# Three hand-written instruction orders laid out anew in a conditional residual MLP

## The chip, the cores and the metric

The kernel runs on one core of one Trainium2 chip. The time is that of the device, in microseconds (us), for one execution. Engines are named as the profile names them: PE (matmul), PEld (PE's weight load), DVE (vector), ACT (scalar), POOL (GpSimd) and SP (which issues most of the plain DMAs).

## The reference

For 16 x 512 tokens of width 512 the reference adds to `x` a two-layer MLP with a layer norm. The MLP's input is the concatenation of six modulated copies of the token, 3072 wide:

```python
h = _ln(x, pw_g[pathway_ids], pw_b[pathway_ids])
h = _ln(h, cp_g[compartment_ids], cp_b[compartment_ids])
t = _ln(x, tm_g[time_steps], tm_b[time_steps])
m = x + _mlp_ln(memory_state, ...)[:, None, :]      # one row per sequence; n and r likewise
s = _ln(x, ms_g[scale_type], ms_b[scale_type])
w = jax.nn.softmax(aw)
cat = jnp.concatenate([w[0]*h, w[1]*t, w[2]*m, w[3]*n, w[4]*r, w[5]*s], axis=-1)
return x + _mlp_ln(cat, int_W1, int_b1, int_W2, int_b2, int_g, int_be)   # _mlp_ln: silu(s@W1+b1)@W2+b2, then layer norm
```

`compartment_ids` and `time_steps` are the same array, with values 0 to 4; `scale_type` is an array of 0 and 1; `pathway_ids` runs from 0 to 499.

## The kernel before

**Tiling.** The tokens are sorted into groups by their compartment and scale, and are worked through in 16 groups `w` of 512 tokens, four tiles of 128 each. Layer 1 multiplies three 512-wide inputs of a token: X (the token itself, row sums folded into per-row additions), V (its normalised form, with weights scaled per compartment and scale) and H (the twice normalised form). Each input is transposed by DVE (`turn`, L198) and spread over the partitions by four DMAs of SP (`spread_row`, L206). Layer 2 (Z is its transposed input) runs one group behind layer 1.

**Products.** The V part of a tile is one piece `lV.w.j` (L405, accumulating into a PSUM tile `p`). X and H of two tiles at a time (pair `p`, 0 or 1) go through seven half products `m7.w.p.k` (`half_product`, L453) instead of eight; four sums of their inputs (`u1` to `u4`, `token_sum`, L434 to L440) and four sums of their outputs (`r1`, `r2`, `r3`, `r5`, `half_out`, L462 to L470) belong to them; products 1, 6, 7 and 5 share a PSUM tile `u`. Layer 2 has the same scheme: fourteen sevenths per group, `q7.w.p.k` (`seventh`, L547), which write two PSUM tiles per pair, `pq_0a`, `pq_0b` for p = 0 and `pq_1a`, `pq_1b` for p = 1. Products 1, 6 and 2 go to the a tile, 5, 3, 7 and 4 to the b tile. Between them the partial results are taken out:

```python
def sum_first(st, i):                                   # piece sf.w.i, L564 (even i) and L566 (odd i)
    y, ab, ed = y_halves(st, i // 2)
    if i % 2 == 0:
        nc.vector.tensor_add(y[:, 0], y[:, 0], ab[:, 1])
    else:
        nc.vector.tensor_add(y[:, 3], y[:, 3], ed[:, 1])
```

`kf` (`keep_first`, ACT, L557 and L559) and `ku` (`keep_last`, ACT, L570) copy a half out, `sl` (`sum_last`, DVE, L575 and L577) makes the last sums, `kb` (ACT, L521) puts the bias into a PSUM tile ahead of the first product, `zs` (`z_sums`, POOL, L533 to L539) makes the sums of the products' inputs. In the last group layer 2 runs as plain products, `l2` (L488).

**Other pieces that the text names.** On POOL the gathers of rows by index (L172): `gx` the tokens, `gh` and `gc` two tables, `ga` the additions to layer 1's result; `sh` (L392); `xp` and `fp` powers; `po` (L639) the scatter of the result. On DVE `f1` (L347, L348), `f2` (L384), `th`, `tx`, `tv`, `tz` the transposes of H, X, V and Z (L198), `ha` the addition to layer 1's result (L473), `wz` the half sums of layer 1's weights (L420 to L423), `wq` those of layer 2's (L495 to L498), `bd.w.j` the build of a V block (L266), which runs only where a tile begins a new sort group and is a skipped branch elsewhere (L249), and the last steps `yg` (L585), `la` (L608), `ft` (L604).

**Order.** Nothing schedules the work but three lists of piece names: `ORDER` (the head: preparation, the three small MLPs of the conditions, group 0's layer 1 and the start of group 1), `WINDOW` (the steady group) and `LAST` (the last group). `run` calls the pieces in the list's order, and each engine gets its instructions in that order. `WINDOW` is run 15 times, with c for the current group, p for the one before, n and m for the next two:

```python
for w in range(NW - 1):
    run(WINDOW, w)
run(LAST, NW - 1)
```

Waits between engines are put in by the tiles that a piece reads and writes: an instruction waits for every earlier one, in the list's order, that read or wrote the tile in a way that conflicts. A PSUM tile of 128 x 512 counts as one tile there, also where two instructions touch different halves of it. Where a list names a reader of a tile ahead of the next product into it, the product waits for the reader; where it names it behind, the reader waits for the product.

Of the kernel before, what the change touches and what calls it, by code (L numbers as in the profile page):

```python
# [1549 lines left out]
```

## Time and profile before

| | |
|---|---|
| median of 3 runs | 920.85 us (915.66 to 922.26) |
| span of the profiled execution | 922.1 us, mean granted clock 0.988 |
| PE busy | 886.5 us, 96% |
| DVE busy | 736.2 us, 80% |
| POOL busy | 656.9 us, 71% |
| ACT busy | 524.5 us, 57% |

The span is counted from the first to the last instruction of the profiled execution; all sums below are made against it. A row of a timeline names start, duration, engine, line, operation, what is written and read, and in brackets the idle time of the engine ahead of it and what ended that. A row of the chain names start, duration and the work. Matmul durations reach past the next one's start, since they are pipelined; a matmul's slot is the distance between two starts.

### The profile page before, as it was taken

The page shows a single profiled execution, that of the slowest core. Times are in us where ns is not written, and L with a number is a line of the kernel's source. Part 1 is how long each engine was busy: PE and PEld are TensorE (multiplying, and loading weights), DVE is VectorE, ACT ScalarE, POOL GpSimd, SP SyncE. Part 2 cuts the span into 40 slices and gives each one's busy share as a digit, 9 for nine tenths or more (in the row PEclk, how much of TensorE's full clock was granted, in tenths as well). Part 3 has the DMA queues.
Part 4 walks back from the last instruction along what each step waited for, and adds up shares of the span by engine and source line. Part 5 has one row for each costly group of instructions (what it writes and reads, how often), then busy time and mean ns, then how long its engine had stood idle before and what let it go on. Part 6 is the DMA issues. An engine that isn't in the chain of part 4 may idle for free.

```text
span 922.1 us, 13747 instructions
## 1 busy us (share of the span) xinstructions
PE 886.5 (96%) x3617; PEld 644.0 (70%) x3617; DVE 736.2 (80%) x1360; ACT 524.5 (57%) x1263; POOL 656.9 (71%) x730
## 2 busy tenths in 40 slices
PE   6978998999999999999999999999999999999995
PEld 6634445868777776767687777778686867778682
DVE  8776866878879798978787887969799798979565
ACT  5558735556473738564564647374657566573313
POOL 9867678566867868687777777786768687866352
PEclk9979999999999999999999999999999999999999
DMA  8836687586867767686868676686768696876513
GB/s 273 276 104 204 216 235 215 151 246 169 246 182 215 209 196 223 183 234 190 250 178 244 185 229 200 203 229 194 214 173 246 168 259 174 246 201 181 152 37 111
DMA packets 88558, 185.40 MB, mean 201 GB/s; under 512 B 24324, under 2 KB 24388, under 8 KB 88476
## 3 DMA queue, kind: packets, MB, share of 16 engines
q0 software_dynamic: 31104, 104.88, 39.7%
q1 hardware_dynamic: 56668, 79.53, 29.1%
q8 instruction: 30, 0.49, 0.3%
q14 instruction: 52, 0.43, 0.2%
q10 hardware_dynamic: 704, 0.08, 0.1%
HBM read 100.48 MB, written 19.97 MB: 131 GB/s over the span
## 4 chain that ended last, share of the span: by engine, by line
PE 46%; POOL 4%; issue 3%; DVE 2%; SPq 1%; DMA 1%; POOLq 0%; ACT 0%; DVEq 0%
PE u L453 12%; PE p L405 12%; PE p L453 10%; PE pq_0b L547 4%; PE pq_1b L547 3%; PE pq_0a L547 2%; PE pq_1a L547 2%; POOL out L639 1%; SPq L206 1%; DMA catZ<-rZ 1%; POOL xbs L392 1%; PE p L488 0%; POOL xbs L172 0%; POOL rsh L373 0%; POOL cp L172 0%
## 5 line engine op out<-in xcount | busy, mean ns | idle before, releaser
L405 PE MATMUL p<-vs,catV 128*128 128x512 f32 x512 | 231.9, 596 | 4.3 <-ACT sums L352 3.6
L405 PEld LDWEIGHTS p<-vs,catV 128*128 128x128 f32 x512 | 97.6, 191 | 103.3 <-issue 96.2
L373 POOL TENSOR_TENSOR rsh<-veh,mhalf 128x1 f32<-128x1 f32 x64 | 52.3, 817 | 84.4 <-DVE veh L369 68.8
L453 PE MATMUL p<-wh__81,catH 128*128 128x256 f32 x480 | 110.9, 379 | 0.0
L377 ACT ACTIVATE pw<-pw,rsh 128x512 f32<-128x512 f32 x64 | 46.0, 718 | 104.4 <-DVE pw L384 55.1
L453 PEld LDWEIGHTS p<-wh__81,catH 128*128 128x128 f32 x480 | 91.2, 190 | 12.4
L639 POOL DMA_INDIRECT out<-yb,tok x64 | 67.8, 1059 | 33.5 <-issue 19.4
L172 POOL DMA_INDIRECT pw<-in_pw,i_pw x64 | 63.0, 984 | 34.8 <-DVE veh L369 20.5
L476 ACT ACTIVATE add<-add 128x512 f32<-128x512 f32 x64 | 40.0, 629 | 82.4 <-DVE add L473 55.1
L172 POOL DMA_INDIRECT add<-rows,i_add x64 | 71.6, 1119 | 20.0 <-issue 18.0
L351 ACT ACTIVATE junk<-pw 128x512 bf16<-128x512 f32 x60 | 37.7, 628 | 80.1 <-DVE pw L348 59.3
L392 POOL TENSOR_TENSOR xbs<-xbs,rows 128x512 f32<-128x512 f32 x64 | 82.1, 1285 | 1.2
L172 POOL DMA_INDIRECT xbs<-in_x,tok x64 | 66.8, 1043 | 17.2 <-issue 14.7
L172 POOL DMA_INDIRECT cp<-cp_rows,i_cp x64 | 67.1, 1048 | 16.2 <-issue 13.2
L347 DVE SCALAR_TENSOR_TENSOR pw<-xbs,sums,pw 128x512 f32<-128x512 f32 x60 | 54.1, 902 | 16.8 <-DMA pw<-in_pw,i_pw 14.3
L384 DVE SCALAR_TENSOR_TENSOR pw<-pw,sumsh,cp 128x512 f32<-128x512 f32 x60 | 43.6, 748 | 28.4 <-DMA cp<-cp_rows,i_cp 20.8
L318 ACT ACTIVATE xm<-xbs,nmx,rsx 128x512 f32<-128x512 f32 x64 | 48.8, 807 | 27.0 <-issue 11.0
L453 PEld LDWEIGHTS u<-wx__80,catX 128*128 128x128 f32 x240 | 45.6, 190 | 18.7 <-issue 13.4
L453 PE MATMUL u<-wt,catX 128*128 128x256 f32 x240 | 56.6, 379 | 0.1
L453 PE MATMUL p<-wt,catH 128*128 128x256 f32 x240 | 56.7, 379 | 0.0
L453 PE MATMUL u<-wx__80,catX 128*128 128x256 f32 x240 | 56.7, 379 | 0.0
L453 PE MATMUL u<-wt,ss 128*128 128x256 f32 x240 | 54.4, 379 | 0.0
(439 smaller groups left out, 2098.0 us busy)
## 6 DMA issues: line engine op xcount, KB each, us to landing
catX<-rX SPq DMA_DIRECT2D x240, 64.0 KB
catV<-rV SPq DMA_DIRECT2D x240, 64.0 KB
catZ<-rZ SPq DMA_DIRECT2D x240, 64.0 KB
catH<-rH SPq DMA_DIRECT2D x240, 64.0 KB
rows<-adde SPq DMA_DIRECT2D x8, 256.0 KB
yb<-in_int_W SPq DMA_DIRECT2D x1, 1024.0 KB
catH<-in_int_W SPq DMA_DIRECT2D x1, 1024.0 KB
w1x<-in_int_W SPq DMA_DIRECT2D x1, 1024.0 KB
```

Source lines behind the costliest of these rows:

```text
L172: nc.gpsimd.indirect_dma_start(dst, None, table, bass.IndirectOffsetOnAxis(ap=idx, axis=0), **kw)
L318: nc.scalar.activation(t, st["xb"][:, j, :], AF.Identity, bias=st["nm"][:, j : j + 1], scale=st["rs"][:, j : j + 1])
L347: nc.vector.scalar_tensor_tensor(h, st["xb"][:, j, :], st["sums"][:, 1, j : j + 1], h, ALU.add, ALU.mult)
L373: nc.gpsimd.tensor_tensor(rs, st.pop(("ve", j)), mhalf[:, :1], ALU.pow)
L377: nc.scalar.mul(pw[:, :D], pw[:, :D], st.pop(("rs", j)))
L384: nc.vector.scalar_tensor_tensor(pw[:, :D], pw[:, :D], st["sh", j][:, 1], cp, ALU.add, ALU.mult)
L392: nc.gpsimd.tensor_add(st["xb"][:, j, :], st["xb"][:, j, :], rows[:, 2, :])
L405: nc.tensor.matmul(st["p1", g], st["c" + blk][:, g, c, :], m[:, c, :], start=(blk == first and c == order[0]), stop=(blk == last and c == ...
L453: nc.tensor.matmul(dst, m[:, c], at_["half1"][k][:, c], start=(k == 1 and c == 0), stop=(c == NC - 1), skip_group_check=True)
L476: nc.scalar.activation(st["add", g], st["add", g], AF.Silu)
L547: nc.tensor.matmul(st["pq", 2 * p + i][:, half], st["zp", p][k][:, c], at_["half"][k][:, c], start=False, stop=(c == 1), skip_group_check= ...
L639: nc.gpsimd.indirect_dma_start(out_rows[j], bass.IndirectOffsetOnAxis(ap=tok[:, j, w : w + 1], axis=0), yb[:, j, :], None)
```

## The change

The three lists are new permutations. Each list holds the names that it held before, in another order, so the same pieces run in both; nothing else in the file differs. The core of the diff, the lines of `WINDOW` around the second pair's sevenths and the lines of `ORDER` that hold wz, in before and after:

```diff
-    sl.p.1 xm.n f1.n.0 q7.p.1.7 q7.p.1.5 m7.c.1.4 q7.p.1.6 nv.n.3 nv.n.1 kf.p.3 tv.n.3 tv.n.1 sf.p.3 q7.p.1.4
+    q7.p.1.6 kf.p.3 nv.n.1 nv.n.3 sl.p.1 sh.c.2 sf.p.2 lq.p.0 sf.p.3 tv.n.1 zs.p.7 q7.p.1.4 f1.n.0 q7.p.1.3
...
-    fn.1.2 th.1.2 wz f1.1.0 bd.1.1 ha.0.3 f1.1.1 ha.0.0 ha.0.1 wl.2 fs.1.0 hs.0.3 hs.0.0 hs.0.1 fs.1.1 fv.1.0
+    fn.1.2 wz ga.0.3 sV.1.1 wm.3 f1.1.0 lH.0.0 th.1.2 ga.0.0 ga.0.2 fs.1.0 lH.0.1 sX.1.3 ha.0.0 ha.0.3 sX.1.2
```

**The steady group, PE.** PE's rows around the last sevenths of a group before (each row holds the two accumulation steps of one seventh, `x4` two sevenths; the row into p_2_3 is m7.c.1.4):

```order
L547 MATMUL pq_0b<-w_82,yb 128x256 x2
L547 MATMUL pq_1b<-w2t,zs_2217 128x256 x2
L547 MATMUL pq_1b<-w_82,catZ 128x256 x2
L453 MATMUL p_2_3_2160<-wt_1589,catH 128x256 x4
L547 MATMUL pq_1a<-w2t,zs_2217 128x256 x2
L547 MATMUL pq_1b<-w2t,catZ 128x256
L249 UNCONDITIONAL_BRANCH
L547 MATMUL pq_1b<-w2t,catZ 128x256
L249 UNCONDITIONAL_BRANCH
L547 MATMUL pq_1b<-w_82,zs_2217 128x256 x2
```

and after:

```order
L547 MATMUL pq_0b<-w_82,yb 128x256 x2
L547 MATMUL pq_1a<-w_82,catZ 128x256 x2
L547 MATMUL pq_0b<-w2t,catZ 128x256 x2
L547 MATMUL pq_1b<-w_82,catZ 128x256 x2
L547 MATMUL pq_1b<-w2t,zs_2190 128x256 x2
L547 MATMUL pq_1a<-w2t,zs_2190 128x256 x2
L547 MATMUL pq_1b<-w2t,catZ 128x256 x2
L547 MATMUL pq_1b<-w_82,zs_2190 128x256 x2
```

q7.p.1.6 is the row that writes pq_1a from zs, q7.p.1.4 the row behind it that writes pq_1b from catZ. m7.c.1.4, which stood ahead of q7.p.1.6, stands later, behind lV.c.2.

**The steady group, DVE.** The same place on DVE before:

```order
L297 TENSOR_SCALAR vea<-sums 128x4
L564 TENSOR_TENSOR yb<-yb,pq_1a 128x256
L575 TENSOR_TENSOR yb<-yb 128x256
L577 TENSOR_TENSOR yb<-yb,pq_0b 128x512
L312 TENSOR_TENSOR nmx<-sums,rsx 128x4
L347 SCALAR_TENSOR_TENSOR pw_0_2210<-xbs_91,sums,pw_0_2210 128x512
L348 SCALAR_TENSOR_TENSOR pw_0_2210<-pw_0_2210,rsx 128x512
L198 STREAM_TRANSPOSE rV_2281<-xm_3_2276 128x4x4x32
L198 STREAM_TRANSPOSE rV_2281<-xm_1_2278 128x4x4x32
L566 TENSOR_TENSOR yb<-yb,pq_1b 128x256
L198 STREAM_TRANSPOSE rV_2281<-xm_2_2298 128x4x4x32
```

and after:

```order
L575 TENSOR_TENSOR yb<-yb 128x256
L198 STREAM_TRANSPOSE rX_2116<-xbs_91 128x4x4x32
L312 TENSOR_TENSOR nmx<-sums,rsx 128x4
L462 TENSOR_TENSOR add_0_2072<-add_0_2072,u_0_2076 128x256
L577 TENSOR_TENSOR yb<-yb,pq_0b 128x512
L564 TENSOR_TENSOR yb<-yb,pq_1a 128x256
L566 TENSOR_TENSOR yb<-yb,pq_1b 128x256
L198 STREAM_TRANSPOSE rV_2269<-xm_1_2259 128x4x4x32
L347 SCALAR_TENSOR_TENSOR pw_0_2188<-xbs_91,sums,pw_0_2188 128x512
L348 SCALAR_TENSOR_TENSOR pw_0_2188<-pw_0_2188,rsx 128x512
L198 STREAM_TRANSPOSE rV_2269<-xm_3_2261 128x4x4x32
```

sf.p.2 is the row L564 on pq_1a, sf.p.3 the row L566 on pq_1b. Before, three other instructions and two transposes lie between them; after, sf.p.3 follows sf.p.2 at once. In the list, sf.p.2 stood ahead of q7.p.1.6 and stands behind it now.

**The end of the head, DVE.** In `ORDER`, th.1.2 stood just ahead of wz on DVE; now it stands behind wz and behind f1.1.0. Around the half sums of layer 2's weights (L495 to L498, wq), before:

```order
L198 STREAM_TRANSPOSE rZ_1620<-add_2_1579 128x4x4x32
L198 STREAM_TRANSPOSE rH_1521<-pw_0_1565 128x4x4x32
L198 STREAM_TRANSPOSE rH_1521<-pw_1_1568 128x4x4x32
L495 TENSOR_TENSOR w2t<-w_82 128x512
L496 TENSOR_TENSOR w_82<-w_82 128x2x256
L497 TENSOR_TENSOR w2t<-w_82 128x512
L249 UNCONDITIONAL_BRANCH
L498 TENSOR_TENSOR w2t<-w_82,w2t 128x512
L249 COMPARE_AND_BRANCH
L266 SCALAR_TENSOR_TENSOR vs_86<-wt,sct,vs_86 128x512 x4
```

The same place after:

```order
L198 STREAM_TRANSPOSE rZ_1605<-add_2_1556 128x4x4x32
L495 TENSOR_TENSOR w2t<-w_82 128x512
L496 TENSOR_TENSOR w_82<-w_82 128x2x256
L497 TENSOR_TENSOR w2t<-w_82 128x512
L498 TENSOR_TENSOR w2t<-w_82,w2t 128x512
L249 UNCONDITIONAL_BRANCH
L198 STREAM_TRANSPOSE rH_1493<-pw_0_1522 128x4x4x32
L198 STREAM_TRANSPOSE rH_1493<-pw_1_1524 128x4x4x32
L249 COMPARE_AND_BRANCH
L266 SCALAR_TENSOR_TENSOR vs_86<-wt,sct,vs_86 128x512 x4
```

The two transposes of pw_0 and pw_1 (th.1.0, th.1.1) stood ahead of wq and stand behind it now, ahead of the branch of bd.1.3.

**The tail, DVE.** Of the last group, before:

```order
L440 TENSOR_TENSOR catH<-catH,ss_7860 128x512
L585 TENSOR_TENSOR yg_0_7890<-yb,rows 128x512
L466 TENSOR_TENSOR add_0_7698<-add_0_7698,u_0_7709 128x256
L467 TENSOR_TENSOR add_1_7764<-add_1_7764,u_0_7709 128x256
L621 TENSOR_SCALAR vey<-ssy 128x1
L438 TENSOR_TENSOR catX<-catX 128x512
L464 TENSOR_TENSOR add_0_7698<-add_0_7698,u_0_7709 128x256
L438 TENSOR_TENSOR catX<-catX 128x512
L621 TENSOR_SCALAR vey<-ssy 128x1
L440 TENSOR_TENSOR catH<-catH,ss_7860 128x512
L466 TENSOR_TENSOR add_2_7762<-add_2_7762,u_1_7790 128x256
L467 TENSOR_TENSOR add_3_7777<-add_3_7777,u_1_7790 128x256
```

and after:

```order
L438 TENSOR_TENSOR catX<-catX 128x512
L466 TENSOR_TENSOR add_0_7774<-add_0_7774,u_0_7725 128x256
L467 TENSOR_TENSOR add_1_7784<-add_1_7784,u_0_7725 128x256
L440 TENSOR_TENSOR catH<-catH,ss_7848 128x512
L464 TENSOR_TENSOR add_0_7774<-add_0_7774,u_0_7725 128x256
L462 TENSOR_TENSOR add_2_7820<-add_2_7820,u_1_7692 128x256
L438 TENSOR_TENSOR catX<-catX 128x512
L466 TENSOR_TENSOR add_2_7820<-add_2_7820,u_1_7692 128x256
L467 TENSOR_TENSOR add_3_7887<-add_3_7887,u_1_7692 128x256
L464 TENSOR_TENSOR add_2_7820<-add_2_7820,u_1_7692 128x256
```

L466 and L467 are the two instructions of r5, L462 is r1, L464 r2, L438 u3. In `LAST`, r5.c.0 stood behind m7.c.1.6 and now stands between m7.c.0.5 and m7.c.0.6; r1.c.1, u3.c.1 and r5.c.1 now stand between m7.c.1.5 and m7.c.1.6; kf.p.3 and kf.p.2, which stood behind q7.p.1.1, now stand between q7.p.1.5 and q7.p.1.2.

More of the change, by code (lines that the diff above doesn't have):

```diff
@@ new lines @@
+    f1.0.1 mt.e0.0 mt.e0.1 lX.0.1 ey.0 nv.e0.3 fs.0.1 ez.0 rp2 ey.1 ex.0 xs.e1.2 gx.1.1 xs.e1.3 gr.e0.2 gx.1.3
+    tx.1.1 nv.e0.2 ea.0 fp.0.2 va.0 wm.0 mt.e0.2 vv.0.0 fn.0.2 ey.2 tx.1.3 gc.0.1 gr.e0.3 ar xe.e1 ee.0 f2.0.1
+    ez.1 gx.1.2 xs.1.3 ht.0.2 hv.0.2 gh.0.3 eo.0 fv.0.1 ez.2 fp.0.1 sp.0.0 mt.e0.3 wm.2 bd.0.0 lV.0.1 xp.e1
+    fn.0.1 tx.1.0 tx.1.2 xs.1.2 ex.2 ey.3 gc.0.3 f1.0.3 ex.1 ht.0.1 gr.e1.0 xm.e1 fs.0.3 f2.0.3 nv.e1.0 xa.1
+    ea.2 gr.e1.2 ea.3 xs.1.1 hv.0.1 fv.0.3 ea.1 nv.e1.2 mt.e1.2 ez.3 mt.e1.0 wm.1 xs.1.0 ey.6 xe.1 ee.2 gh.1.3
@@ new lines @@
+    nv.e1.3 fp.0.3 gr.e1.3 fn.0.3 ey.4 ex.3 sp.0.3 gr.e1.1 xp.1 ee.1 ht.0.3 nv.e1.1 mt.e1.1 ez.6 eo.2 ee.3 ez.4
+    ey.5 gh.1.2 xm.1 eo.1 mt.e1.3 ez.5 nv.1.1 ea.5 ea.7 ex.4 eo.3 ex.5 ey.7 gc.1.3 ex.6 ea.4 ea.6 ez.7 bd.0.3
+    wl.2 sX.1.1 ee.6 eo.6 f1.1.3 ex.7 f1.1.2 lV.0.0 sp.0.2 wl.0 tv.1.1 bd.0.2 gc.1.2 fs.1.3 fv.1.3 f2.1.3 nv.1.0
+    tv.1.0 wl.1 fs.1.2 lX.0.3 fp.1.3 hv.0.3 lV.0.3 ee.5 fn.1.3 lV.0.2 ee.4 sX.1.0 ee.7 fv.1.2 th.1.3 sp.1.0
+    nv.1.2 eo.4 sh.0.0 lH.0.3 gc.1.0 nv.1.3 fp.1.2 tv.1.3 bd.1.0 eo.5 tv.1.2 gh.1.0 gh.1.1 sh.1.2 eo.7 f2.1.2
@@ L63 @@
+    tz.c.0 gx.m.3 po.p.2 po.p.3 hs.c.3 tz.c.1
 """
 LAST = """
[L66 to L69 removed]
@@ new lines @@
+    q7.p.0.2 gc.c.3 f1.c.3 sZ.p.1 sh.c.3 fs.c.3 fv.c.2 f2.c.2 bd.c.2 sZ.p.3 sp.c.3 fp.c.2 fv.c.3 fp.c.3 ga.c.0
+    q7.p.0.1 bd.c.3 f2.c.3 ga.c.1 fn.c.2 zs.p.0 kf.p.0 sZ.p.2 zs.p.1 zs.p.2 fn.c.3 zs.p.3 lV.c.2 zs.p.4 q7.p.0.5
+    q7.p.0.7 th.c.2 th.c.3 sH.c.0 sH.c.2 q7.p.0.6 ga.c.2 kf.p.1 sf.p.1 q7.p.0.4 r1.c.0 ku.p.0 q7.p.0.3 lV.c.3
+    sH.c.3 sl.p.0 sl.p.1 sf.p.0 sH.c.1 lq.p.1 u1.c.0 u2.c.0 m7.c.1.2 zs.p.5 u1.c.1 m7.c.0.2 u2.c.1 lq.p.0
+    m7.c.1.4 u3.c.0 sh.c.1 m7.c.0.5 r5.c.0 m7.c.0.6 kb.p.2 m7.c.1.5 u4.c.1 r2.c.0 ga.c.3 r1.c.1 sh.c.0 u3.c.1
@@ new lines @@
+    r5.c.1 m7.c.1.6 r2.c.1 u4.c.0 vr.p.0 vr.p.1 m7.c.0.7 m7.c.1.7 zs.p.6 m7.c.1.3 r3.c.0 kb.p.3 r3.c.1 ha.c.3
+    m7.c.0.4 yg.p.0 zs.p.7 pr.p.0 ha.c.2 hs.c.3 tz.c.3 hs.c.2 ft.p.0 pr.p.1 m7.c.0.3 tz.c.2 ha.c.1 q7.p.1.1
+    q7.p.1.7 hs.c.1 ha.c.0 tz.c.1 q7.p.1.5 hs.c.0 tz.c.0 sZ.c.0 yg.p.1 kf.p.3 sf.p.3 kf.p.2 ft.p.1 q7.p.1.2 w2
+    q7.p.1.6 q7.p.1.3 sZ.c.2 ku.p.1 q7.p.1.4 l2.c.0 sf.p.2 sl.p.2 e0 sl.p.3 sZ.c.1 po.p.0 lq.p.3 yg.p.2 l2.c.2
+    sd.p.3 lq.p.2 sd.p.2 la.c.0 l2.c.1 yg.p.3 po.p.1 rv.p.2 sh.c.2 lq.c.0 ft.p.2 sd.c.0 sZ.c.3 l2.c.3 rv.c.0
```

75 lines of the change are left out of this document (27 added, 48 removed).

## The prediction

> **What bounds the kernel now.** I read first the page's forty slices and the windows of 23 us, then the chain that ended last, then PE's timeline wherever a window was not full.
>
> From the windows (us; PE, PEld, DVE, ACT and POOL busy; PEclk, DMA share, GB/s), three of the head, two of the steady groups, and one of ten us:
>
> ```profile
> 46.00:69.00 23.00, 17.58 (x108) 9.15 (x108) 16.16 (x51) 12.27 (x28) 14.62 (x13) 0.78 0.32 104
> 115.00:138.00 23.00, 22.43 (x54) 9.75 (x53) 15.56 (x19) 8.91 (x18) 17.21 (x16) 1.00 0.81 234
> 138.00:161.00 23.00, 19.43 (x60) 11.41 (x59) 14.86 (x22) 12.26 (x29) 19.83 (x22) 0.93 0.76 215
> 506.00:529.00 23.00, 23.00 (x93) 17.24 (x92) 17.94 (x38) 16.21 (x41) 16.06 (x19) 1.00 0.68 191
> 644.00:667.00 23.00, 21.63 (x77) 14.19 (x76) 16.55 (x29) 14.76 (x39) 16.76 (x19) 1.00 0.76 210
> 150.00:160.00 10.00, 7.99 (x21) 4.69 (x22) 4.20 (x5) 4.34 (x13) 8.66 (x11) 0.83 0.75 208
> ```
>
> In the steady part PE is full, at a clock of 1.00. The chain there is nothing but PE, and two starts of the same product (lV.c.1) in neighbouring groups give the group's length:
>
> ```profile
> 495.76 3.43 PE p L405 x8
> ...
> 528.49 6.91 PE u L453 x32
> ...
> 545.75 3.43 PE p L405 x8
> ```
>
> 545.75 less 495.76 is 49.99 us. That is all matmul slots: 4 x 3.43 (L405), 14 x 6.91/4 = 1.73 (L453) and 14 half as long (L547: same width, half the passes) make 50.0. Order alone cannot bring a steady group below 50.0. What it can win there is what is lost beyond that:
>
> ```profile
> 193.67 1.88 PE L405 MATMUL p<-vs,catV 128*128 128x512 f32 x4
> ...
> 847.39 3.17 PE L405 MATMUL p<-vs,catV 128*128 128x512 f32 x7
> ```
>
> 13 groups between these starts take 653.7 us, 3.7 over 13 x 50.0. So there is almost nothing to win in 71% of the span, and everything to lose: any new wait of PE counts in full, once per group.
>
> **The steady group: the main term.** In the lists of before, sf.p.2 (L564, reads pq_1a) stands ahead of the seventh q7.p.1.6 (writes pq_1a), and m7.c.1.4 fills 1.73 us of PE ahead of that seventh. In the new list q7.p.1.6 comes first, sf.p.2 behind it, sf.p.3 (L566, reads pq_1b) behind that on DVE, and PE's next seventh, q7.p.1.4, writes pq_1b. Since a PSUM tile counts as one, this is a loop of waits: sf.p.2 for the end of q7.p.1.6, q7.p.1.4 for the end of sf.p.3. PE has nothing between the two sevenths. The prices, all from before's trace (PE first, then ACT and DVE):
>
> ```profile
> 512.80 1.03 PE L547 MATMUL pq_0a<-w2t,yb 128*128 128x256 f32 x4
> ...
> 520.57 1.03 PE L547 MATMUL pq_1a<-w2t,zs 128*128 128x256 f32 x4
> 521.44 1.03 PE L547 MATMUL pq_1b<-w2t,catZ 128*128 128x256 f32 x4
> ```
>
> ```profile
> 513.87 0.37 ACT L570 COPY yb<-pq_0a 128x256 f32<-128x256 f32 x1 [0.26 <-PE pq_0a L547]
> ...
> 515.85 0.35 ACT L557 COPY yb<-pq_1a 128x256 f32<-128x256 f32 x1
> ```
>
> ```profile
> 516.23 0.42 DVE L564 TENSOR_TENSOR yb<-yb,pq_1a 128x256 f32<-128x256 f32 x1
> 516.57 0.42 DVE L575 TENSOR_TENSOR yb<-yb 128x256 f32<-128x256 f32 x1
> ...
> 520.67 0.38 DVE L566 TENSOR_TENSOR yb<-yb,pq_1b 128x256 f32<-128x256 f32 x1
> ```
>
> And what a stall of PE looks like (DVE, then PE):
>
> ```profile
> 420.91 0.38 DVE L566 TENSOR_TENSOR yb<-yb,pq_1b 128x256 f32<-128x256 f32 x1
> ```
>
> ```profile
> 421.35 0.92 PE L547 MATMUL pq_1b<-w2t,catZ 128*128 128x256 f32 x3
> ```
>
> ```profile
> 259.98 1.13 PE L547 MATMUL pq_0b<-w2t,yb 128*128 128x256 f32 x4 [0.67 <-POOL yb L533]
> ```
>
> ```profile
> 662.59 1.13 PE L547 MATMUL pq_0b<-w2t,yb 128*128 128x256 f32 x4 [1.37 <-POOL yb L533]
> ```
>
> A seventh ends 0.16 us after its slot (520.57 + 1.03 against 521.44); the reader starts 0.04 later (512.80 + 1.03 = 513.83, ACT at 513.87); sf.p.2 takes 0.34 until the next DVE instruction starts (516.23 to 516.57), sf.p.3 0.38; PE starts 0.06 behind DVE (421.29 to 421.35); and the first seventh after a stall is 0.10 longer (1.13 against 1.03). 0.16 + 0.04 + 0.34 + 0.38 + 0.06 + 0.10 = 1.08 us. It falls due for p = 0 to 13, 14 times: 15.1 us. The Trainium skill (VectorE: DVE Perf Modes, "The DRAIN you can't avoid") says that the next DVE operation does not start until the pipe is empty; by that sf.p.3 would start 0.08 us later, and the sum would be 1.1 us higher. The rows disagree (516.57 lies ahead of 516.23 + 0.42 = 516.65), so I keep 0.34.
>
> Against it stand the 3.7 us that before loses. Both large losses are waits for POOL's z_sums (L533); in the new list sZ.p.* and the first z_sums stand earlier, so I take all 3.7 back. Other covers in the new group are thin: zs.p.6, zs.p.7 stand behind xp.n and sh.c.2 on POOL, kb.p.3 just ahead of q7.p.1.5, sf.p.1 just ahead of q7.p.0.4. By the same durations each holds by 0.2 to 1 us; where a group builds its block (bd.n.1) one may not: I add 1.5 in all, bounds 0 and 6. Below zero is excluded, PE being full. Steady: 15.1 - 3.7 + 1.5 = +12.9 (11.4 to 17.4).
>
> **The head.** PE's largest gaps, the row from which the steady groups count, and the pieces that set it (PE, DVE, POOL):
>
> ```profile
> 49.77 1.09 PE L1213 MATMUL ptX<-ident,xbs 128*128 128x128 f32 x4 [4.31 <-DMA xbs<-in_x,tok]
> ...
> 137.53 3.60 PE L405 MATMUL p<-vs,catV 128*128 128x512 f32 x8
> ...
> 152.01 5.37 PE L405 MATMUL p<-vs,catV 128*128 128x512 f32 x8 [3.57 <-ACT sums L352]
> ```
>
> ```profile
> 123.73 1.18 DVE L420 TENSOR_TENSOR wt<-wh__81,wx__80 128x1024 f32<-128x1024 f32 x1
> ...
> 128.48 1.23 DVE L423 TENSOR_TENSOR wt<-wh__81,wt 128x1024 f32<-128x1024 f32 x1
> ...
> 146.59 0.65 DVE L495 TENSOR_TENSOR w2t<-w 128x512 f32<-128x512 f32 x1
> ...
> 148.72 3.13 DVE L498 TENSOR_TENSOR w2t<-w,w2t 128x512 f32<-128x512 f32 x1
> ```
>
> ```profile
> 124.08 1.68 POOL L172 DMA_INDIRECT pw<-in_pw,i_pw  x1 [0.54 <-DVE rH L198]
> ...
> 137.13 1.24 POOL L172 DMA_INDIRECT add<-rows,i_add  x1 [0.16 <-issue]
> ```
>
> Up to lV.1.1 (137.53) the new list puts small products ahead of the token transposes that wait 4.31 at 49.77. At best that gap goes whole, and with it the slow clock behind it: 0.22 x 23 = 5.1 us in 46:69. At worst nothing is won. I take 5 of 9.4, near the middle: lV.1.1 at 132.5. Behind it the new list gives back: gh.1.1 (POOL, 124.08) waits for th.1.2, which now stands behind wz (123.73 to 129.71, 5.98) on DVE, not ahead of it, and four gathers follow gh.1.1. With wz from about 117, the turn behind it is done at 125, and the last gather ends near 133.5, not 138.37. wq (146.59 to 151.85) needs what stands ahead of it; as far behind the last gather as before (8.2) it runs 141.7 to 147.0. Now th.1.0 and th.1.1 stand behind it, 0.7 each, and only then bd.1.3, for which lV.1.3 waits (the page names ACT, but PE starts 0.16 after L498 ends): 148.5 to 149.5. So of 5 us 2.6 are left, and PE's gap ahead of lV.1.3 grows by about 2. Bounds: -9.4, all won and kept; +2, if the gather chain is later than I place it.
>
> **The tail.** The new last group has the same kind of loop: r5.15.0 (L466, L467) stands between m7.15.0.5 and m7.15.0.6, which writes the same u; r1, u3 and r5 of pair 1 between m7.15.1.5 and m7.15.1.6; kf.14.3, kf.14.2 between q7.14.1.5 and q7.14.1.2.
>
> ```profile
> 882.91 0.42 DVE L466 TENSOR_TENSOR add<-add,u 128x256 f32<-128x256 f32 x1 [0.44 <-PE u L453]
> 883.25 0.41 DVE L467 TENSOR_TENSOR add<-add,u 128x256 f32<-128x256 f32 x1
> ```
>
> ```profile
> 894.69 1.10 PE L547 MATMUL pq_1a<-w2t,zs 128*128 128x256 f32 x4 [0.60 <-ACT yb L557]
> ```
>
> ```profile
> 915.69 0.75 DVE L604 SCALAR_TENSOR_TENSOR yb<-yg,sd,xbs 128x512 f32<-128x512 f32 x1
> 915.79 1.49 POOL L639 DMA_INDIRECT out<-yb,tok  x1 [1.89 <-DVE sd L597]
> 917.58 0.96 POOL L639 DMA_INDIRECT out<-yb,tok  x1 [0.30 <-issue]
> ```
>
> The first costs 0.36 around it (as above) + 0.34 + 0.41 = 1.1; the second, with r1 and u3 ahead, about 2.0; the third 0.36 + two copies of 0.35 = 1.05. 4.1 in all, of which 0.70 replace the wait at 894.69: +3.4. At the end the last scatter starts at 917.58, 1.14 after the last result (915.69 + 0.75), behind a scatter of 1.49; in the new list the earlier scatters stand earlier, and about 1.6 goes (bounds 0 and 2). Tail +1.8 (0 to +4).
>
> **Rivals.** (a) The head pays for the groups. If the gap at 49.77 and the slow clock go whole (-9.4) and lV.1.3 comes on its slot (-3.57, and 1.7 for the clock of 0.83 in 150:160), the head wins up to 14.7, and the end is 922.1 - 14.7 + 12.9 + 1.8 = 922.1; with two thirds of it, 927. It decides from a head gain of 14.7 on. For it: the gaps are there. Against: bd.1.3 still stands behind wq. (b) Faster: the loop of waits is not there as I read it (sf.p.2 is let through on an earlier product), so 15.1 falls away: 922.1 - 3.7 + 1.5 - 2.6 + 1.8 = 919, and with (a)'s head 907. (c) The clock. A gap of 3.57 left 0.83 in 150:160. If the gap of 1 us, once per group, did the same for ten us, 14 x 1.7 = 24 us more: 957. The windows speak against: in 644:667 a gap of 1.37 left 1.00. The Trainium skill (TensorE: Matmul & The Clock Gate, "A second HAM failure mode: psum-queue depth-cycling") tells of frequent micro-idles that make the clock swing; the trace has no regular ones, and shows it for single gaps only. (d) The thin covers fail in every group, 0.4 more each: 939.
>
> **How the numbers follow.** 922.1 - 2.6 + 12.9 + 1.8 = 934.2 for the profiled execution, which lies 1.25 above the median of 920.85; so 933. Its own range is 925 to 943 (bounds of the three terms, not all at one end). About 1% can be told from no change: 911.6 to 930.1. Forecast 0.65, of which 0.10 lies below 930.1; (a) 0.20, of which 0.03 lies above it; (b) 0.05, of which 0.03 is faster; (c) 0.03; (d) 0.07. Slower 0.55 + 0.03 + 0.03 + 0.07 = 0.68; same 0.10 + 0.17 + 0.02 = 0.29; faster 0.03. The range 922 to 943 leaves out (b), (c), the best fifth of (a) and 0.05 at the forecast's ends, 0.17 in all.
>
> **What would show it.** Right: once in each of 14 groups a L547 seventh into pq_1b with 0.8 to 1 us idle ahead of it, released by DVE L566; L564 on pq_1a waiting for PE L547; starts of lV.c.1 51.1 us apart; PEclk 1.00 there; lV.1.3 near 149; in the tail L453 waiting for DVE L467. Wrong: neighbouring groups 50.0 apart, or lV.1.3 before 143.

## The result: 2.95% slower

The changed kernel takes 946.84 us (median of 4 runs, 946.36 to 948.86) against 919.51 us (915.66 to 922.26) for the kernel before: a ratio of 1.0295, with a 95% interval of 1.0249 to 1.0341. The forecast was 933 with a range of 922 to 943. Its direction was right and its size was not: the time lies 13.8 us above it and outside the range.

The span of after's profiled execution is 944.6 us, against 922.1. Split at four of PE's rows, the 22.5 us lie as follows (all in us):

| stretch of PE's timeline | before | after | difference | forecast |
|---|---|---|---|---|
| start to lV.1.3 | 152.01 | 154.96 | +2.95 | -2.6 |
| lV.1.3 to the last group's first row | 695.38 | 710.67 | +15.29 | +12.9 |
| last group up to layer 2's last products (l2, L488) | 51.36 | 57.44 | +6.08 | +3.4 |
| from there to the end | 23.35 | 21.53 | -1.82 | -1.6 |

The medians differ by 27.3, not by 22.5. In every experiment below the time of a profiled execution lies 1.7 to 2.5 above its span, so before's profiled execution took about 924, more than any of the four timed runs above. Its head was a late one; the section on the hardware shows a part of the reason. The table therefore understates what the new head costs.

**The steady group.** PE's timeline of after, the two starts of lV.c.1 that answer to those shown of before, and the wait between them:

```profile
505.80 3.60 PE L405 MATMUL p<-vs,catV 128*128 128x512 f32 x8
...
529.06 1.03 PE L547 MATMUL pq_1a<-w2t,zs 128*128 128x256 f32 x4
...
530.98 1.13 PE L547 MATMUL pq_1b<-w2t,catZ 128*128 128x256 f32 x4 [0.90 <-DVE yb L566]
...
556.97 3.60 PE L405 MATMUL p<-vs,catV 128*128 128x512 f32 x8
```

The group is 556.97 - 505.80 = 51.17 long, where it was 49.99. Between q7.p.1.6 (529.06) and q7.p.1.4 (530.98) PE stands idle for 0.90. DVE's timeline at that place, and the line of after's waits that sums them (us in total, times, longest):

```profile
530.18 0.42 DVE L564 TENSOR_TENSOR yb<-yb,pq_1a 128x256 f32<-128x256 f32 x1 [0.42 <-ACT yb L559]
530.51 0.42 DVE L566 TENSOR_TENSOR yb<-yb,pq_1b 128x256 f32<-128x256 f32 x1
```

```profile
PE pq_1b L547 <- DVE yb L566: 12.6, 14, 0.9
```

The seventh ends at 529.06 + 1.03 = 530.09, sf.p.2 (L564) starts at 530.18, sf.p.3 (L566) ends at 530.93, and PE goes on at 530.98. (The bracket names ACT as the releaser of L564; the times say it was PE's seventh.) The wait is there 14 times. The windows of after show that the clock stays at 1.00 beside it (columns as in the prediction; the third last is the granted clock):

```profile
506.00:529.00 23.00, 23.00 (x84) 15.62 (x83) 15.93 (x27) 16.20 (x42) 18.79 (x21) 1.00 0.78 225
529.00:552.00 23.00, 22.10 (x95) 17.68 (x94) 20.81 (x40) 10.56 (x25) 14.44 (x14) 1.00 0.62 181
```

**The head.** After's PE, then the pieces that set it on DVE and POOL:

```profile
122.60 13.90 PE L405 MATMUL p<-wh__81,catH 128*128 128x512 f32 x32
141.47 5.37 PE L405 MATMUL p<-vs,catV 128*128 128x512 f32 x8 [4.98 <-ACT add L476]
...
154.96 3.67 PE L405 MATMUL p<-vs,catV 128*128 128x512 f32 x8 [0.59 <-ACT junk L353]
```

```profile
122.44 1.22 DVE L420 TENSOR_TENSOR wt<-wh__81,wx__80 128x1024 f32<-128x1024 f32 x1
...
129.07 0.70 DVE L198 STREAM_TRANSPOSE rH<-pw 128x512 f32<-128x512 f32 x1
138.58 1.29 DVE L473 TENSOR_TENSOR add<-p,add 128x512 f32<-128x512 f32 x2 [8.80 <-issue]
...
140.56 0.75 DVE L348 SCALAR_TENSOR_TENSOR pw<-pw,rsx 128x512 f32<-128x512 f32 x1
```

```profile
130.04 0.95 POOL L172 DMA_INDIRECT pw<-in_pw,i_pw  x1 [8.07 <-DMA catV<-rV]
132.45 0.98 POOL L172 DMA_INDIRECT add<-rows,i_add  x1 [0.16 <-issue]
...
136.26 0.96 POOL L172 DMA_INDIRECT add<-rows,i_add  x1 [0.30 <-issue]
```

lV.1.1 could have started at 141.47 - 4.98 = 136.49, 1.0 ahead of its start in before (137.53). It starts 3.9 behind it. On DVE the new list has ha.0.0 and ha.0.3 (L473) and f1.1.1 (L348) ahead of bd.1.1, a skipped branch for which lV.1.1 waits. ha waits for rows that POOL gathers; in after's order the gathers stand behind gh.1.1 (130.04), which waits for th.1.2 (129.07), and that stands behind wz (122.44). The skipped branch, which needs none of this, comes free when L348 ends at 141.31, and lV.1.1 starts 0.16 later. That the branch is what holds lV.1.1, and how much th.1.2 matters, is tested below.

**The tail.** The waits of PE that the profile lists in after's last group:

```profile
877.54 1.97 PE L547 MATMUL pq_0a<-w,catZ 128*128 128x256 f32 x8 [1.43 <-ACT vs L258]
...
896.61 2.00 PE L453 MATMUL u<-wx__80,ss 128*128 128x256 f32 x8 [0.42 <-DVE ss L434]
899.93 2.00 PE L453 MATMUL u<-wt,ss 128*128 128x256 f32 x8 [1.32 <-DVE add L467]
905.43 2.00 PE L453 MATMUL u<-wt,ss 128*128 128x256 f32 x8 [1.78 <-DVE add L467]
919.51 1.13 PE L547 MATMUL pq_1a<-w,catZ 128*128 128x256 f32 x4 [0.87 <-ACT yb L557]
923.07 13.90 PE L488 MATMUL p<-w,catV 128*128 128x512 f32 x32
```

The last three are the three loops that the prediction priced. The first two it did not name.

### The profile page after: what moved, and what is told of

It is laid out like the page before. It is cut to its first block, busy times and chain, and to the rows that moved or that the text cites. A ratio compares the mean times of both kernels' runs of the same rounds, so it can differ in the third digit from the quotient of the medians.

```text
span 944.6 us, 13668 instructions
## 1 busy us (share of the span) xinstructions
PE 894.2 (95%) x3617; PEld 643.9 (68%) x3617; DVE 748.8 (79%) x1360; ACT 525.3 (56%) x1263; POOL 657.3 (70%) x730
## 5 line engine op out<-in xcount | busy, mean ns | idle before, releaser
L639 POOL DMA_INDIRECT out<-yb,tok x64 | 71.4, 1115 | 28.9 <-issue 18.0
L384 DVE SCALAR_TENSOR_TENSOR pw<-pw,sumsh,cp 128x512 f32<-128x512 f32 x60 | 59.8, 1017 | 27.4 <-DMA cp<-cp_rows,i_cp 27.4
L172 POOL DMA_INDIRECT add<-rows,i_add x64 | 63.7, 995 | 16.9 <-issue 14.5
L626 POOL TENSOR_TENSOR rsy<-vey,mhalf 128x4 f32<-128x4 f32 (+1 forms) x16 | 21.9, 1369 | 75.4 <-DVE vey L621 75.4
L453 PE MATMUL u<-wt,ss 128*128 128x256 f32 x240 | 57.0, 381 | 3.1 <-DVE add L467 3.1
L453 PE MATMUL u<-wx__80,ss 128*128 128x256 f32 x240 | 56.8, 380 | 0.4 <-DVE ss L434 0.4
```

Source lines behind the costliest of these rows:

```text
L172: nc.gpsimd.indirect_dma_start(dst, None, table, bass.IndirectOffsetOnAxis(ap=idx, axis=0), **kw)
L384: nc.vector.scalar_tensor_tensor(pw[:, :D], pw[:, :D], st["sh", j][:, 1], cp, ALU.add, ALU.mult)
L453: nc.tensor.matmul(dst, m[:, c], at_["half1"][k][:, c], start=(k == 1 and c == 0), stop=(c == NC - 1), skip_group_check=True)
L626: nc.gpsimd.tensor_tensor(st["rsy"][:, lo:hi], st["vey", lo], mhalf[:, lo:hi], ALU.pow)
L639: nc.gpsimd.indirect_dma_start(out_rows[j], bass.IndirectOffsetOnAxis(ap=tok[:, j, w : w + 1], axis=0), yb[:, j, :], None)
```

## The experiments

Three questions are open after this. Do the parts add up, list by list? Is the loop of sf.p.2 and sf.p.3 the whole reason for the longer group? And what in the head costs the time, and could it be had back? In the experiments' files the lists are wrapped differently, so that a line may stand one or two numbers lower than in before and after (L546 or L545 for L547). All times are compared with runs of the kernel before on the same chip, whose medians lay between 919.1 and 919.7. No kernel leaves out work; a name that stands in `ORDER` and again in `WINDOW` runs once, at its first place.

### One list at a time: head, steady group, tail

The new `ORDER` alone, with `WINDOW` and `LAST` of before:

```diff
 ORDER   as in after
-WINDOW, LAST   as in after
+WINDOW, LAST   as in before
```

> The new head with the steady and last lists of before. Theory (the head loses by itself, by the wait ahead of lV.1.1): lV.1.1 starts near 141.5, not 137.5, lV.2.1 about 1.5 to 2.7 us later than before's 193.7, and the time is 1.5 to 3 us above before. Rival (the head is neutral, and what the trace shows there belongs to the steady list's first group): lV.2.1 within 0.5 us of before, time the same.

The new `WINDOW` alone:

```diff
 WINDOW   as in after
-ORDER, LAST   as in after
+ORDER, LAST   as in before
```

> The new steady list with the head and last lists of before. Theory (the three parts add up; the steady list carries most): plain groups 51.17 apart, the groups with block builds 1 to 2.5 longer, lV.2.1 to lV.15.1 17 to 18 us longer than before, time 16 to 19 above before, 936 to 939. Rival (much of the loss is made only together with the new head or last list): less than 12 above before.

The new `LAST` alone:

```diff
 LAST   as in after
-ORDER, WINDOW   as in after
+ORDER, WINDOW   as in before
```

> The new last list with the head and steady lists of before. Theory (the tail loses by itself: waits of PE 6.1 more, end 1.8 shorter): from lV.15.1 or its neighbour to the end 4.3 us longer than before, time 4 us above before. Rival (the waits at the last group's start, 1.4 at the first q7.14 products, come from where the new steady list leaves the other engines): about 2 us above before.

| alone | us | ratio to before (95%) | us more |
|---|---|---|---|
| head | 925.9 (924.88 to 927.13) | 1.007 (1.0052 to 1.0088) | +6.3 |
| steady group | 938.72 (936.65 to 941.44) | 1.0205 (1.0175 to 1.0236) | +19.6 |
| tail | 921.55 (918.54 to 925.27) | 1.0024 (1.0007 to 1.0041) | +2.0 |

They add up to 27.9 us; the whole change costs 27.3. The intervals leave some 2 to 3 us either way for each, so a small exchange between the parts can't be excluded, but no large one: the head's loss isn't taken up by the groups, nor the groups' by the tail. The head, forecast as a gain of 2.6, is a loss of 6.3 in time, more than the 1.5 to 3 expected of this run; the tail came out as its rival said. PE's row of the run with the new head alone shows the same wait as after (L348 takes 1.95 there and ends at 142.65, again 0.16 ahead of lV.1.1):

```profile
142.81 5.10 PE L404 MATMUL p<-vs,catV 128*128 128x512 f32 x8 [5.84 <-issue]
```

The tail alone shows the three loops (0.84, 1.78 and 0.87) but no wait of 1.43 at the first seventh of the last group. The new steady list alone doesn't show it either: with before's `LAST` two more V products stand ahead of this seventh, and it starts 17.2 behind the last group's first row (863.61 and 880.79 in that run), where its slot in after lies 10.5 behind it. The wait comes where both new lists meet. The bracket names ACT's build of a block, which this seventh doesn't read; what it does read is Z. The last of Z's four transposes on DVE and SP's issue of Z's transfers in after:

```profile
871.75 0.70 DVE L198 STREAM_TRANSPOSE rZ<-add 128x512 f32<-128x512 f32 x1
```

```profile
872.52 7.89 SPq L206 DMA_DIRECT2D catZ<-rZ  x11
```

and with the tail alone SP's issue and the same seventh on PE:

```profile
846.33 10.04 SPq L204 DMA_DIRECT2D catZ<-rZ  x16
```

```profile
851.66 1.89 PE L545 MATMUL pq_0a<-w,catZ 128*128 128x256 f32 x8
```

There the seventh starts 5.33 behind the first transfer and does not wait. In after its slot (877.54 - 1.43 = 876.11) lies 3.59 behind it, and it starts 5.02 behind it. So it is Z's transfers that fit; SP begins them 0.07 after the last transpose. The new steady list brings them later relative to PE's products: 6.9 behind the last group's first row in after (865.63) and 7.1 with the new steady list alone, but 5.1 with the tail alone (841.20). The run further below that covers the loop's wait bears this out: there SP begins 8.2 behind that row (867.52 against 859.29), the same seventh waits longer, the bracket names Z's transfer, and the seventh again starts 5.1 behind the first of them:

```profile
872.64 3.24 PE L546 MATMUL pq_0a<-w,catZ 128*128 128x256 f32 x8 [2.09 <-DMA catZ<-rZ]
```

No run moved the transposes alone.

### The loop: turn the wait round, or cover it

If sf.p.2's wait for q7.p.1.6 were the whole cause, putting q7.p.1.6 behind sf.p.2 in the list would remove the loop:

```diff
 WINDOW
-zs.p.6 q7.p.1.6 kf.p.3 nv.n.1 nv.n.3 sl.p.1 sh.c.2 sf.p.2 lq.p.0 sf.p.3
+zs.p.6 kf.p.3 nv.n.1 nv.n.3 sl.p.1 sh.c.2 sf.p.2 q7.p.1.6 lq.p.0 sf.p.3
```

> The changed kernel with one name moved in the steady list: q7.p.1.6 behind sf.p.2. Every engine keeps its own order of work; only who waits for whom at one PSUM tile is turned round (q7.p.1.6 waits for sf.p.2, not sf.p.2 for q7.p.1.6). Theory of the loop: the idle time at q7.p.1.4 falls from 0.90 to about 0.2 us (kf.p.3 and sf.p.3 behind q7.p.1.7 are left), neighbouring groups stand 50.3 apart in place of 51.17, and the time falls by 12 us to about 934. Rival, thin covers: another piece of the new order is nearly as late, the idle time moves to another row of PE, groups stay at 51 or more and the time falls by less than 3 us.

948.56 us (945.49 to 949.88), 1.0312 (1.0287 to 1.0338): not faster than after. Its PE and DVE timelines say why:

```profile
531.43 1.10 PE L546 MATMUL pq_1a<-w2t,zs 128*128 128x256 f32 x4 [1.02 <-DVE yb L563]
```

```profile
529.34 0.69 DVE L311 TENSOR_TENSOR nmx<-sums,rsx 128x4 f32<-128x4 f32 x1 [0.32 <-POOL rsx L300]
529.95 0.41 DVE L461 TENSOR_TENSOR add<-add,u 128x256 f32<-128x256 f32 x1
530.28 0.68 DVE L576 TENSOR_TENSOR yb<-yb,pq_0b 128x512 f32<-128x512 f32 x1
530.88 0.41 DVE L563 TENSOR_TENSOR yb<-yb,pq_1a 128x256 f32<-128x256 f32 x1
```

The wait has moved one seventh up, and is 1.02. sf.p.2 (L563) no longer waits for q7.p.1.6, but it stands on DVE behind xm.n (L311, which waits 0.32 for POOL's xp.n), r1.c.0 (L461) and sl.p.1 (L576), and this chain lets it start at 530.88, 0.47 behind the slot of q7.p.1.6 (531.43 - 1.02 = 530.41). So two chains end within half a microsecond of each other (in after DVE stood idle for 0.42 ahead of sf.p.2), and breaking one brings the other to light. The theory that the loop is the sole cause falls.

If so, breaking both should shorten the group. sf.p.2 was moved to where DVE is early, ahead of q7.p.1.6 and of xm.n, and sf.p.3 ahead of sl.p.1; kf.p.2 (ACT), which sf.p.2 needs, moved ahead of it; head and tail are those of before:

```diff
 WINDOW (after's)
-q7.p.1.7 sl.p.0 tx.n.2 xm.n kf.p.2 r1.c.0 sH.c.3 zs.p.6 q7.p.1.6 kf.p.3 nv.n.1 nv.n.3 sl.p.1 sh.c.2 sf.p.2 lq.p.0 sf.p.3 tv.n.1
+q7.p.1.7 kf.p.2 sl.p.0 sf.p.2 tx.n.2 xm.n r1.c.0 sH.c.3 zs.p.6 q7.p.1.6 kf.p.3 nv.n.1 nv.n.3 sf.p.3 sl.p.1 sh.c.2 lq.p.0 tv.n.1
```

> Head and last lists of before; the new steady list with three names moved: kf.p.2 behind q7.p.1.7, sf.p.2 behind sl.p.0 (so ahead of tx.n.2 and xm.n on DVE, and ahead of q7.p.1.6), sf.p.3 behind nv.n.3 (ahead of sl.p.1). Theory of two chains (turning the one wait round won nothing because sf.p.2 stands on DVE behind xm.n, which waits for POOL, and behind r1.c.0 and sl.p.1): with both undone the idle time at the sevenths of pair 1 falls from 0.90 to 0.2 to 0.3 us, plain groups stand 50.2 to 50.4 apart, and what is left of the loss against before is the groups in which V blocks are built: 3 to 6 us in all, time 922 to 926. Rival (whatever is moved on DVE, another piece of this order comes late): plain groups stay above 51.

927.55 us (924.5 to 929.8), 1.008 (1.0049 to 1.0111). Beside the new steady list alone (938.72) three pieces in other places win 11 us. What is left of the wait in a plain group, in PE's timeline of this run:

```profile
519.11 1.13 PE L545 MATMUL pq_1b<-w2t,catZ 128*128 128x256 f32 x4 [0.18 <-DVE yb L564]
```

Plain groups are 50.45 long, and like the time just above what was expected; those that build a block still take 50.6 to 52.2.

The third way leaves the loop and puts work into it: lV.c.2 (one slot of 3.43) between the two sevenths, where m7.c.1.4 had stood before in front of both.

```diff
 WINDOW
-q7.p.1.6 kf.p.3 nv.n.1
+q7.p.1.6 lV.c.2 kf.p.3 nv.n.1
...
-sl.p.2 nv.n.2 lV.c.2 tv.n.2
+sl.p.2 nv.n.2 tv.n.2
```

> The changed kernel with one name moved in the steady list: lV.c.2 (3.43 us of PE) between q7.p.1.6 and q7.p.1.4; the loop of waits stays. Theory of the loop: what costs is only that PE has nothing between the two; with the cover the idle time goes whole, groups stand 50.0 to 50.1 apart, and the time falls by 15 us to about 931. Rival, thin covers: idle time shows up at another row and less than 5 us are won.

942.94 us (941.38 to 944.85), 1.0263 (1.024 to 1.0285). The cover works: plain groups fall to 50.09, which over 14 groups is some 15 us. But the run is only 3.9 us faster than after, as the rival said (less than 5, idle time at other rows), though not in every group. The groups with a build now take 50.3 to 54.7, with waits that aren't there in a plain group. From lV.2.1 to the last group's first row (196.46 and 859.29) this run loses 11.7 over 13 plain groups; after loses 4.0 (196.39 and 865.63, against 51.17). The last group, up to l2, is another 2.0 longer than after's, with the wait for Z shown above. Two of the waits of a group with a build, in PE's timeline of this run:

```profile
370.82 1.10 PE L546 MATMUL pq_1b<-w,catZ 128*128 128x256 f32 x4 [0.84 <-issue]
...
381.82 1.97 PE L452 MATMUL p<-wh__81,catH 128*128 128x256 f32 x8 [1.28 <-DMA catH<-rH]
```

After has the same two in the same group (0.84 at 372.63 and 0.89 at 384.40), some time behind a build of 4.15 us on DVE (L266, at 363.09). It may be that in after a wait of 0.9 in every group leaves DVE, POOL and SP as much time to catch up, and that the builds' lateness shows where it is covered. That is an argument and not shown: which piece each of these waits goes back to was not followed further.

### The head: the branch, the gathers, the weight sums

First the skipped branch: bd.1.1, with the piece sp.1.1 that it needs, ahead of ha, in the kernel with the new head alone.

```diff
 ORDER (after's; WINDOW, LAST as in before)
-lH.0.1 sX.1.3 ha.0.0 ha.0.3 sX.1.2 sp.1.1 hs.0.0 f1.1.1 bd.1.1 ga.0.1
+lH.0.1 sX.1.3 sp.1.1 bd.1.1 ha.0.0 ha.0.3 sX.1.2 hs.0.0 f1.1.1 ga.0.1
```

> Steady and last lists of before; the new head with sp.1.1 and bd.1.1 moved ahead of ha.0.0. Theory (lV.1.1 was late only because bd.1.1, a skipped branch, stands on DVE behind ha.0.0 and ha.0.3, which wait for the gathers): lV.1.1 starts on its slot, near 137, not 142. The gathers are as late as in the new head, so wq ends near 152 to 154 and lV.1.3 waits instead: lV.1.3 near 154 to 156, nothing won at lV.2.1 (within 1 us of the new head alone). Rival (lV.1.1 waits for something else, its own DMAs): lV.1.1 stays near 142.

927.02 us (925.27 to 927.72), 1.0065 (1.0043 to 1.0086). PE:

```profile
136.71 3.60 PE L403 MATMUL p<-vs,catV 128*128 128x512 f32 x8
...
154.77 6.16 PE L403 MATMUL p<-vs,catV 128*128 128x512 f32 x8 [7.15 <-ACT junk L351]
```

lV.1.1 comes on its slot: the branch, moved here with sp.1.1, was what held it. And nothing is won, since PE then waits 7.15 at lV.1.3, which starts at 154.77, in the new head alone at 156.07. That wait has its own cause, wq on DVE and the gathers ahead of it. So the second edit also takes th.1.2 out from behind wz:

```diff
 ORDER (with the edit above)
-f2.1.2 fn.1.2 wz ga.0.3
+f2.1.2 fn.1.2 th.1.2 wz ga.0.3
...
-f1.1.0 lH.0.0 th.1.2 ga.0.0 ga.0.2
+f1.1.0 lH.0.0 ga.0.0 ga.0.2
```

> As the one before it, and th.1.2 moved ahead of wz. Theory (gh.1.1 on POOL, and the four gathers behind it, wait for th.1.2): gh.1.1 starts near 124.5, not 130; ha.0.0 near 134, not 138.6; wq ends 4 to 5 us earlier, lV.1.3 near 150, lV.2.1 3 to 5 us earlier than in the new head alone. Rival (POOL itself is the limit there): the gathers move by less than 2 us.

925.79 us (923.91 to 926.14), 1.0048 (1.0022 to 1.0074). The gather gh.1.1 starts at 124.69 instead of 130.04, but lV.1.3 still comes only at 153.94, not near 150. The first gather of additions now waits for a transfer, and wq's last step is caught by POOL (POOL, then DVE):

```profile
131.29 1.34 POOL L170 DMA_INDIRECT add<-rows,i_add  x1 [3.31 <-DMA catV<-rV]
...
148.31 3.70 POOL L390 TENSOR_TENSOR xbs<-xbs,rows 128x512 f32<-128x512 f32 x3
```

```profile
148.16 4.41 DVE L496 TENSOR_TENSOR w2t<-w,w2t 128x512 f32<-128x512 f32 x1
```

So the last gather ends at 136.4 here and at 137.2 in after: th.1.2's place behind wz costs the gathers 0.8 us and not the 4 to 5 expected. Before, where gh.1.1 is early too, has the same wait:

```profile
130.89 1.13 POOL L172 DMA_INDIRECT add<-rows,i_add  x1 [3.52 <-issue]
```

The first gather of additions begins near 131 in both, however early gh.1.1 is. By the program the gathers read rows that SP stores (rows<-adde, issued until about 124.6 here); whether it is these stores that they wait for was not tested.

The same question in the kernel before, where lV.1.3 waits 3.57 behind wq: its branch bd.1.3 ahead of wq.

```diff
 ORDER (before's)
-sH.1.1 sh.0.1 wq
+sH.1.1 sh.0.1 kz.0.0 lV.1.1 sp.1.3 bd.1.3 wq
```

> The kernel before, with lV.1.1, sp.1.3 and bd.1.3 (and kz.0.0) moved ahead of wq at the head's end. Theory (lV.1.3 waits in before for wq's L498, which takes 3.1 to 4.4 us when it runs beside POOL's L392 and 0.7 when it does not; with the branch ahead of it that costs PE nothing): no idle time ahead of lV.1.3 in any run, lV.2.1 near 189.5, not 193.7, median 2 to 4 us below before, and less spread. Rival (what follows, the first sevenths, needs wq as well and waits in its place): idle time moves to the first q7.0 products, no gain.

919.42 us (917.86 to 923.71), 1.000 (0.9983 to 1.0017): no change. lV.1.3 starts on its slot, and in the profiled execution, the slowest of the ten, the wait comes back, 2.59 long, at the next product that needs what DVE and POOL have not yet done:

```profile
148.80 3.60 PE L404 MATMUL p<-vs,catV 128*128 128x512 f32 x8
...
156.71 1.13 PE L546 MATMUL pq_0b<-w2t,yb 128*128 128x256 f32 x4 [2.59 <-POOL yb L532]
```

### Parts for a better version

Only the end of the new `LAST` had been a gain (-1.82 in the trace). Alone, in the kernel before:

```diff
 LAST (before's, from l2.c.0 on; the start of the two orders)
-l2.c.0 ku.p.1 sl.p.2 sl.p.3 sf.p.2 yg.p.3 yg.p.2 la.c.0 lq.p.3 lq.p.2 sd.p.3 sd.p.2 lq.c.0
+l2.c.0 sZ.c.2 ku.p.1 sf.p.2 sl.p.2 sl.p.3 sZ.c.1 lq.p.3 yg.p.2 l2.c.2 sd.p.3 lq.p.2 sd.p.2
...
-e1 lq.c.3 sd.c.3 po.c.1 rv.c.3 ft.c.3 po.c.2 po.c.3
+ft.c.1 sd.c.2 rv.c.2 po.c.0 la.c.3 ft.c.2 po.c.1 yg.c.3 lq.c.3 sd.c.3 rv.c.3 ft.c.3 po.c.2 po.c.3
```

> The kernel before with the new last list's order behind l2.c.0 alone. Theory (the end behind the last waits of PE is the one part of the new order that gains): from the start of l2.15.0 to the end 1.6 to 1.8 us less, time 1.5 to 2 us below before. Rival (the shorter end is hidden, the last scatter waits for the last product anyway): less than 0.5 us.

917.87 us (910.97 to 922.72, 12 runs), 0.9975 (0.9949 to 1.0001). In the trace the stretch from l2 to the end falls from 23.35 to 21.64, as expected; in time 2.3 us less can't be told from no change.

Two more runs put the branch of bd.1.3 and the first z sum of the head ahead of wq, with the end above; the first of them also moves zs.p.0, one of POOL's z sums in the steady group, which PE waits for twice in before:

```diff
 ORDER (before's)
-sH.1.3 sH.1.0 sh.1.1 sH.1.1 sh.0.1 wq
+sH.1.3 sH.1.0 sH.1.1 kz.0.0 lV.1.1 ga.1.0 ga.1.2 zs.0.0 sp.1.3 bd.1.3 wq zs.0.1 zs.0.2 sh.1.1 sh.0.1
 WINDOW (before's)
-sZ.p.2 fp.c.2 ga.c.2 fp.c.3 zs.p.0 lV.c.3
+sZ.p.2 fp.c.2 zs.p.0 ga.c.2 fp.c.3 lV.c.3
```

> The kernel before with what the comparison taught: lV.1.1, sp.1.3, bd.1.3 ahead of wq; ga.1.0, ga.1.2 and zs.0.0 on POOL ahead of sh.1.1 and sh.0.1, so that no L392 runs beside wq's L498; zs.p.0 ahead of ga.c.2 in the steady list; behind l2.c.0 the new last list's order. Theory: L498 takes 0.7 us, no idle time ahead of lV.1.3 nor the first q7.0 products (lV.2.1 near 189, 4 us earlier than in the profiled run of before); the waits for L533 fall from 3.7 to below 1.5 us; the end after l2.c.0 is 1.6 to 1.8 shorter. 4 to 8 us below before, 912 to 916. Rival (each gain comes back as the next wait, as when the branch alone was moved): within 2 us of before.

The second run is the same without the edit of `WINDOW`:

```diff
 WINDOW
-sZ.p.2 fp.c.2 zs.p.0 ga.c.2 fp.c.3 lV.c.3
+sZ.p.2 fp.c.2 ga.c.2 fp.c.3 zs.p.0 lV.c.3
```

> The same end, and at the head's end lV.1.1, sp.1.3, bd.1.3 ahead of wq and ga.1.0, ga.1.2, zs.0.0 on POOL ahead of sh.1.1 and sh.0.1; the steady list is before's. Theory: the groups are as before (lV.2.1 to lV.15.1 653 to 654 us), lV.2.1 2 to 4 us earlier, the end 1.7 shorter; 3 to 5 us below before, 914 to 916. Rival (what the steady list of before lost in the last experiment came from the head's new order, not from zs.p.0): groups stay above 51.

With zs.p.0 moved: 938.0 us (933.79 to 943.33), 1.0201 (1.0169 to 1.0232). Without: 919.02 us (916.84 to 922.2), 0.9998 (0.9981 to 1.0015). Neither comes to the gain that was expected of it. One piece, moved ahead of one gather, costs 19 us: from lV.2.1 to lV.15.1 the first run takes 674.0, the second 651.6. POOL in the first of the two, and PE behind it:

```profile
618.45 0.72 POOL L531 TENSOR_TENSOR yb<-catZ 128x256 f32<-128x256 f32 x1 [2.23 <-DMA catZ<-rZ]
...
620.94 0.72 POOL L533 TENSOR_TENSOR catZ<-catZ 128x256 f32<-128x256 f32 x1
```

```profile
621.71 1.13 PE L545 MATMUL pq_0b<-w,catZ 128*128 128x256 f32 x4 [1.16 <-POOL catZ L533]
```

zs.p.0 waits 2.23 for the transfer of Z. The gather ga.c.2, which could have run in that time, follows it, and the next sum, zs.p.1 (L533 in this file, L535 in before), comes late; PE waits for that one, 11.8 us in 12 places. No version tried is measurably faster than the kernel before.

## Why the prediction came out too low

The head is the step that failed most; in the steady stage it is the term for the groups that build a block, and in the tail two waits that were not named. By the prediction's own steps, in the order of its sum:

- **What bounds the kernel: right.** PE was full in the steady groups, and each new wait of PE counted in full, once per group. The three lists' costs add (27.9 against 27.3).
- **The loop of waits: right in place and count, 8% short in price.** It said 1.08 us per group and 51.1 between starts; measured are 1.16 to 1.17 and 51.17. The reader starts 0.09 behind the seventh, not 0.04; sf.p.3 holds its tile for 0.42, not 0.38; sf.p.2 took 0.33 (0.34), PE's start 0.05 (0.06), the refill 0.10. 14 x 0.08 is 1.1 us.
- **That the loop is the whole cause: wrong, without effect on the sum.** DVE's chain through xm.n and sl.p.1 would have held sf.p.2 until 0.42 ahead of the same moment. The prediction followed the pieces that name the tile and not the other pieces ahead of the reader on its engine.
- **3.7 taken back, 1.5 added: the term that failed in this stage.** The waits for L533 did shrink (one of 0.95 in after), but the groups that build a block lose 4.0 in after, where 1.5 had been added. The bounds of 0 to 6 held it; the value was too near their lower end. Part of this stage's agreement is luck: of the 14 waits the table shows 13, since before's own stretch from lV.1.3 to lV.2.1 was long (41.66, with lV.1.3 at a low clock; after's is 41.43 with the wait in it). In time the new steady list alone costs 19.6, against the 12.9 forecast.
- **The head: the step that failed.** It was forecast at -2.6 and cost +6.3 in time (+2.95 between the two traces). Four links broke. The gap at 49.77 did go, but lV.1.1's slot came only 1.0 earlier (136.49 against 137.53), not 5. Of the 4.31, 2.9 were left by L1307 (62.19 against 65.06), and between there and lV.1.1 the new order has waits of its own, the longest 2.32 at 108.79. The gathers ended at 137.2, not 133.5. The prediction let them follow gh.1.1 at once, but before's own row at 130.89 has them wait for something else, so even a wz that began "from about 117" (it began at 122.44) would have won little. The working looked at wq ahead of bd.1.3, and not at ha and f1.1.1 ahead of bd.1.1, where the same pattern cost 4.98. That is not the sole cause either: with this branch moved the loss came back at lV.1.3 (7.15). And wq took the long form of L498 (4.43), for which it had 3.13 in the price of before. The bounds of -9.4 to +2 didn't reach the truth. (Among PE's largest gaps the prediction left out the longest, 7.2 at L811; it is the same in both kernels.)
- **The slow clock behind the gap: wrong.** The gap is gone in after, and the clock isn't any faster (0.50 from 40 to 50); in before it was low ahead of the gap already, as the last section shows.
- **The tail: right for what it priced, but two waits were left out.** The three loops were put at 1.1, 2.0 and 1.05. Counted as there, with 0.16 of overhang and 0.10 of refill added to the idle time, they came at 1.58, 2.04 and 1.13; with the new `LAST` alone the first was 1.10 and PE's tail grew by 3.4, as forecast. Behind the new steady list the waits of 1.43 and 0.42 are added, and the first loop is longer. The end gave back 1.82 (1.6 forecast).
- **The baseline.** 922.1 was taken as a usual span, and the forecast time was set 1.25 below the forecast span. A time lies some 2 us above its span; that of before's median run would be near 917.5, so 922.1 stood some 4 us too high.

The miss between the traces is 2.4 (steady) + 5.55 (head) + 2.45 (tail and end) = 10.4 of the 13.8. The other 3.4 are that step from span to time: 1.2 were taken off, and after's median lies 2.2 above the span of its trace.

Of the rivals, (a), the head that pays, and (b), no loop, are out. (c), a clock that swings, is out: it stands at 1.00 in the windows with the wait, so the trace doesn't show here what the Trainium skill (TensorE: Matmul & The Clock Gate, "A second HAM failure mode: psum-queue depth-cycling") tells of frequent short idle times. (d), thin covers, came true in the groups with builds only. Of the signs named for a right forecast, the waits at pq_1b, the 51.1, the clock and the waits for L467 came; lV.1.3 stood at 154.96, not near 149.

## What to carry to other kernels

When a list decides the order, read for each piece that PE waits for not only what it needs but what stands ahead of it on its engine, skipped branches included; a cheap piece behind one that waits for a gather inherits the whole wait. Where two chains end close together, breaking one wins nothing, and a stall that goes uncovers the next one, so price a moved piece by the second-latest wait as well. And before one trace is taken as the baseline, its span should be held against the timed runs.
